# Another order table, and other durations in the planner, for a one-core transformer block

## The chip, the cores and the metric

The kernel runs on 1 core of one Trainium2 chip. A time is the device time of one execution in microseconds (us). An execution's time is a little longer than its span, which goes from the first to the last instruction of the trace. Five engines work side by side and meet at semaphores: TensorE (PE; its weight loads are shown apart as PEld), VectorE (DVE), ScalarE (ACT), GpSimd (POOL) and SyncE (SP), which here only issues transfers; its queue is shown as SPq.

## The reference

All is float32; x has 8 sequences of 512 tokens and 128 features. Cut to what matters:

```python
# attention: 16 heads of 64, 8 groups of keys and values, causal, all 512 tokens
q, k, v = x @ W_Q, x @ W_K, x @ W_V
probs = softmax(where(causal, q @ k.T / 8, -1e6))
x = layernorm(x + (probs @ v) @ W_out + b_out)
y = x
for l in range(2):                       # local layers
    h = shift_token(y)                   # half of the features come from the token before
    q, k, v = split(h @ wqkv[l], 3)      # 8 heads of 64
    q, k = rotary_xpos(l2norm(q) * qs[l], l2norm(k) * ks[l])
    # windows of 64 tokens, each sees itself and the window before, causal and at most 64 back
    y = y + local_softmax_attention(8 * q, k, v) @ wo[l]
    h = layernorm(shift_token(y)) * lg[l] + lb[l]
    a, g = split(h @ w1[l] + b1[l], 2)   # 341 each
    y = y + (a * gelu(g)) @ w2[l] + b2[l]
out = layernorm(x + y)
```

## The kernel before

**Steps.** The kernel first writes its work down as 5889 steps and emits nothing. A step is a call of `op(engine, us, fn, r=, w=, lat=, hold=, mode=)`: the engine, a listed duration, a function that emits some instructions, the buffers that it reads and writes, for a transfer the time until it has landed (`lat`), and for TensorE a tiling of the array (`mode`: WHOLE, ROWS, COLS or QUADS). `Plan.op` derives from the buffers which steps need which. There are 1264 steps on TensorE, 1744 on VectorE, 1384 on ScalarE, 993 on GpSimd and 504 on SyncE.

**The order.** `ORDER` is a table with the 5889 numbers of the steps, every one once. `Plan.run` walks it and calls each step's function; the tile framework's own scheduling is off (`manual_schedule`). So each engine gets its instructions in the order in which the table has its steps, and each engine works strictly in that order, SyncE's queue of transfers too. What an instruction has to wait for follows from the data and buffers, not from the table.

**Buffers.** `Plan.run` also keeps a small model of time. It uses the listed durations, `HOP` (a time per engine between a producer's end and the start of its reader), `TAIL` and `SWITCH`. This model does one thing in the emitted program: where a step needs a new buffer (one of 8 PSUM banks, or one of a few slots of a class such as `two`, `four`, `p3T`, `dram`), it takes the one that the model says is free first. Nothing is delayed or timed by it when the program runs.

**The stages of one sequence (a "batch", b = 0 to 7).** Attention: `heads` projects keys, queries and values (L828, L834, L843) for a pair of groups. `results` goes over the queries in three groups of 128-token tiles, (3), (2) and (0, 1): scores (L883, ROWS), mask and row minimum on VectorE (L895), exponentials with their sum on ScalarE (L907), reciprocal on VectorE (L915), normalization on GpSimd (L922). The weights must then be transposed. For tile pair (0, 1), and for all tiles of batch 0, TensorE does it (L935) and ScalarE or VectorE copies it back (L942). For tiles 3 and 2 of batches 1 to 7 VectorE transposes blocks of 32 x 32 (L957), a transfer stores them in DRAM (`leave`, L800) and four transfers read them back with the blocks in their new places (`come`, L804). Then come the values (L976, COLS), the output projection (L995) and a norm (`norm_rows`: transposition L754, statistics on VectorE L762 to L765, power on GpSimd L768, scaling on VectorE L775; `features` transposes back, L786).

Two local layers follow (`layer`): values (L1033), queries and keys (L1056), squares (L1063), norms, rotary (L1102, L1109, L1116, L1122 on VectorE and GpSimd), a transposition as above (L1156, L800, L804; in the last batch on TensorE, L1136), scores (L1183 and L1198, QUADS), softmax (L1219, L1224, L1230, L1232), transposition of the weights on TensorE (L1239, copied by L1242), outputs (L1251, COLS), projection (L1264), a norm, the feed-forward part (gate L1288, GELU L1295, other half L1303 with L1306, second matrix L1313 with L1319). At the end x is added (L1328), normed and stored (L1331).

The table interleaves the batches: the next batches' attention stands between the local layers of the batches before, and at the end of the table only batch 7 is left.

Of the kernel before, what the change touches and what calls it, by code (L numbers as in the profile page):

```python
# [16 lines left out]
PE, DVE, ACT, POOL, SP = range(5)  # L17
# [23 lines left out]
class Plan:  # L41
# [4 lines left out]
    HOP = (0.055, 0.034, 0.034, 0.085, 0.05)  # L46
# [91 lines left out]
    0, 66, 67, 258, 68, 76, 1, 82, 2, 12, 69, 7, 78, 77, 11, 13, 6, 9, 8, 10, 63, 80, 79, 83, 174,  # L138
    175, 187, 200, 194, 259, 808, 81, 215, 188, 16, 176, 177, 201, 195, 228, 241, 189, 207, 208, 32,
    28, 181, 190, 170, 235, 202, 216, 182, 56, 222, 203, 229, 223, 224, 191, 166, 178, 204, 49, 236,  # L140
    19, 183, 209, 184, 179, 210, 74, 171, 237, 180, 14, 196, 242, 230, 168, 72, 185, 225, 211, 3,
    226, 248, 238, 167, 197, 231, 73, 70, 192, 217, 218, 198, 169, 75, 27, 193, 199, 232, 186, 212,
    243, 233, 249, 2262, 219, 71, 220, 205, 206, 221, 172, 234, 173, 213, 244, 239, 250, 245, 240,
    251, 252, 53, 246, 18, 247, 138, 139, 227, 145, 40, 253, 22, 140, 125, 141, 142, 126, 46, 214,
    151, 158, 254, 127, 128, 143, 809, 132, 146, 159, 147, 152, 153, 129, 43, 110, 4, 144, 50, 97,
    160, 161, 148, 84, 154, 64, 111, 262, 104, 133, 134, 21, 155, 130, 135, 255, 47, 98, 85, 149,
    51, 810, 99, 86, 91, 92, 100, 162, 136, 263, 163, 156, 41, 87, 131, 137, 105, 117, 150, 106,
    260, 118, 157, 101, 93, 813, 119, 88, 112, 102, 89, 90, 103, 94, 164, 107, 113, 814, 95, 120,
    121, 122, 114, 115, 116, 108, 292, 165, 96, 52, 299, 109, 266, 293, 300, 267, 301, 294, 268,
    279, 286, 302, 295, 296, 123, 287, 280, 273, 303, 124, 320, 288, 289, 333, 307, 281, 23, 274,  # L150
    304, 269, 20, 270, 282, 327, 25, 297, 334, 335, 321, 322, 290, 291, 314, 275, 323, 283, 5, 276,
    315, 328, 44, 336, 340, 324, 256, 341, 325, 308, 329, 330, 316, 317, 284, 277, 309, 326, 271,
    310, 337, 342, 343, 278, 298, 331, 338, 272, 318, 344, 311, 332, 261, 285, 2989, 257, 305, 319,
    312, 345, 17, 45, 313, 339, 415, 422, 65, 423, 389, 306, 390, 416, 424, 59, 346, 402, 348, 396,
    391, 392, 24, 374, 425, 409, 417, 397, 393, 410, 403, 398, 418, 361, 29, 811, 55, 15, 355, 404,
    347, 349, 399, 419, 57, 362, 411, 412, 356, 357, 358, 405, 394, 264, 350, 375, 406, 413, 351,
    368, 363, 265, 395, 369, 352, 420, 58, 426, 427, 407, 815, 400, 414, 376, 364, 365, 370, 381,
    421, 359, 408, 816, 353, 371, 372, 401, 377, 812, 382, 366, 367, 428, 383, 378, 384, 373, 354,
    379, 380, 385, 61, 360, 62, 839, 844, 840, 386, 387, 827, 832, 866, 429, 388, 841, 878, 845,
    846, 842, 847, 60, 828, 833, 883, 884, 867, 885, 879, 868, 54, 871, 430, 829, 48, 42, 843, 848,  # L160
    872, 830, 1535, 26, 831, 851, 431, 38, 873, 834, 432, 880, 881, 823, 835, 890, 849, 886, 858,
    859, 882, 433, 852, 853, 825, 434, 897, 860, 861, 1536, 874, 909, 824, 898, 1537, 869, 435, 862,
    436, 870, 821, 437, 438, 887, 836, 891, 899, 888, 900, 439, 819, 854, 447, 892, 837, 37, 850,
    838, 875, 445, 893, 826, 855, 894, 876, 901, 456, 455, 453, 820, 454, 457, 910, 485, 889, 863,
    448, 561, 487, 446, 486, 562, 36, 488, 449, 856, 857, 895, 817, 450, 493, 489, 877, 902, 496,
    822, 525, 913, 451, 533, 490, 495, 914, 452, 458, 818, 864, 494, 918, 527, 526, 896, 491, 915,
    865, 937, 916, 497, 459, 919, 925, 944, 460, 920, 903, 534, 945, 930, 926, 528, 529, 563, 921,
    927, 440, 946, 931, 938, 904, 939, 964, 952, 461, 492, 463, 917, 928, 922, 441, 932, 976, 965,
    969, 966, 929, 911, 933, 947, 970, 934, 957, 1540, 530, 531, 566, 958, 977, 912, 907, 498, 948,
    971, 978, 983, 564, 959, 923, 967, 940, 532, 953, 972, 954, 535, 536, 968, 979, 935, 481, 565,  # L170
    905, 949, 2263, 955, 960, 499, 956, 462, 924, 908, 936, 464, 980, 941, 984, 906, 973, 482, 572,
    974, 961, 537, 538, 1541, 471, 567, 568, 942, 981, 569, 521, 943, 985, 950, 982, 465, 2264, 575,
    472, 574, 573, 962, 1001, 986, 473, 474, 1006, 501, 466, 467, 1025, 539, 522, 468, 1013, 951,
    1007, 987, 444, 570, 442, 500, 975, 1032, 995, 443, 963, 988, 484, 1002, 475, 541, 1008, 476,
    1003, 469, 1018, 1019, 1014, 1004, 1015, 1016, 1009, 1005, 1552, 989, 1026, 1020, 503, 470, 996,
    1017, 502, 990, 477, 1021, 1033, 1010, 1052, 540, 1022, 1053, 1034, 543, 1064, 1071, 478, 576,
    1040, 1054, 1057, 1023, 1065, 1058, 504, 511, 1059, 1045, 1538, 542, 1055, 1066, 1041, 571, 577,
    479, 1072, 991, 1073, 1011, 1056, 1027, 1028, 505, 1029, 480, 1042, 1035, 1043, 1067, 1060,
    1046, 1047, 523, 1539, 1061, 578, 1036, 512, 1048, 1074, 993, 1037, 1553, 1030, 994, 544, 513,
    1024, 1044, 1049, 1031, 545, 1012, 524, 483, 506, 551, 1038, 1062, 992, 514, 546, 552, 1079,  # L180
    1080, 1081, 1084, 1103, 553, 1068, 1091, 1085, 580, 507, 1092, 1093, 1050, 1063, 1104, 1082,
    1051, 31, 547, 1086, 1087, 1105, 999, 579, 508, 1546, 35, 515, 1069, 1083, 1110, 1070, 1075,
    997, 582, 1076, 1096, 1106, 1097, 1077, 1000, 516, 509, 1098, 1094, 1095, 1088, 1039, 998, 1118,
    1078, 1142, 510, 1089, 1099, 1100, 1101, 1123, 1130, 1111, 1119, 517, 554, 1124, 1135, 1107,
    1108, 1547, 581, 1112, 1125, 1126, 1136, 1131, 1542, 1113, 1149, 1143, 1120, 1132, 1144, 1543,
    1090, 1724, 555, 1109, 1102, 1121, 1122, 1114, 1133, 1636, 1550, 1137, 30, 1115, 1145, 1134,
    1127, 556, 1128, 1146, 1147, 1138, 1139, 1725, 518, 1148, 1140, 1150, 583, 584, 1116, 1551,
    1554, 590, 1151, 591, 1578, 592, 1555, 1129, 548, 1117, 1566, 1637, 585, 593, 1579, 1152, 1556,
    1634, 1153, 1585, 1544, 1635, 1154, 594, 1141, 1155, 1567, 1568, 586, 1557, 1558, 1559, 1569,
    549, 1605, 1571, 1560, 1572, 1570, 1586, 595, 1561, 1562, 1593, 1563, 1545, 1587, 1573, 1574,  # L190
    1156, 1610, 1575, 1594, 1580, 1617, 550, 587, 1581, 1618, 1588, 1624, 1625, 1598, 1599, 1564,
    1157, 1626, 1576, 39, 1565, 1158, 1582, 1583, 1600, 1595, 1596, 1611, 1589, 1590, 1606, 588,
    1159, 1601, 1612, 519, 1160, 589, 1607, 557, 1584, 596, 1577, 558, 1161, 33, 1597, 1613, 1162,
    1591, 1163, 1691, 1619, 520, 1164, 1608, 1602, 1592, 1627, 1609, 1614, 1603, 1679, 1166, 1615,
    1696, 1165, 1692, 1703, 1680, 597, 1693, 1620, 559, 1174, 1697, 1694, 1684, 1685, 560, 1695,
    1698, 1172, 1173, 1704, 1181, 1621, 1681, 1699, 598, 1175, 1686, 599, 1700, 1604, 1710, 1622,
    1548, 601, 1628, 600, 1167, 602, 1682, 1687, 1182, 1705, 1683, 1616, 1623, 1629, 1183, 603,
    1208, 1180, 1214, 1711, 1688, 1689, 1176, 604, 1712, 605, 1168, 1630, 1549, 1212, 1209, 1184,
    1177, 1631, 1652, 1215, 1701, 1702, 1664, 1640, 1178, 1213, 1653, 1690, 1706, 1654, 606, 1657,
    1179, 1658, 1671, 1672, 1641, 1185, 607, 1659, 1660, 1655, 1642, 1645, 1656, 1632, 1713, 1248,  # L200
    1665, 609, 1210, 1646, 1252, 1186, 610, 1643, 1647, 1644, 1714, 1249, 1648, 1666, 1673, 1638,
    1633, 1216, 1217, 608, 1187, 1707, 1661, 1715, 1649, 1260, 1218, 1639, 1708, 1253, 1188, 1709,
    1223, 1674, 612, 1716, 1211, 1222, 611, 1221, 1220, 1662, 1219, 1261, 1650, 1728, 1740, 613,
    1733, 1752, 1667, 1734, 1224, 1254, 1717, 1745, 1729, 1746, 1741, 1189, 1668, 1753, 614, 1262,
    1669, 1675, 1747, 1759, 1255, 1263, 1730, 1760, 1722, 1735, 1225, 1226, 1670, 1256, 1264, 616,
    1190, 1191, 1736, 1742, 1743, 1744, 1192, 1676, 1663, 617, 1754, 1755, 1731, 1732, 1756, 1651,
    1228, 1198, 1193, 1748, 1677, 2265, 1678, 2266, 1779, 1169, 615, 1723, 1791, 1784, 1199, 1792,
# [293 lines left out]
def kernel(  # L501
# [21 lines left out]
    nc = tc.nc  # L523
# [875 lines left out]
```

## Time and profile before

| | us |
|---|---|
| median of 3 runs | 1192.32 (1189.94 to 1193.11) |
| the profiled execution | 1189.79 |
| its span | 1188.0 |
| TensorE busy in the span | 1154.2 (97%) |
| VectorE, ScalarE, GpSimd busy | 952.6 (80%), 959.6 (81%), 891.4 (75%) |

The granted TensorE clock is 0.997 of full speed over the span. The transfers move 173.23 MB, at a mean of 146 GB/s.

How to read it: a row of groups shows the line, the engine, the operation, what it writes and reads, how often, its busy time, the mean of one in ns, and the idle time of the engine just before it with what ended that. A row of waits ("engine line <- what it waited for") shows the total in us, how often, and the longest. [...]

### The profile page before, as it was taken

How to read it: one execution, taken by the hardware profiler on the slowest of the kernel's cores; microseconds unless marked ns; L12 is line 12 of the kernel's file. 1: busy time of each engine (PE TensorE's matmuls, PEld its weight loads, DVE VectorE, ACT ScalarE, POOL GpSimd, SP SyncE). 2: the span in 40 equal slices, each digit the busy share in tenths (PEclk: the TensorE clock that was granted, in tenths of full speed). 3: DMA queues.
4: the chain of work that ended last, by engine and by line, in shares of the span. 5: the costliest groups of instructions: out<-in, count | busy, mean ns of one | idle time of the engine just before them, and what ended most of it. 6: DMA issues, size and time to landing. Idle time of an engine off the chain costs nothing.

```text
span 1188.0 us, 32813 instructions
## 1 busy us (share of the span) xinstructions
PE 1154.2 (97%) x11024; PEld 769.2 (65%) x11024; DVE 952.6 (80%) x2988; ACT 959.6 (81%) x3049; POOL 891.4 (75%) x1391
## 2 busy tenths in 40 slices
PE   8999999999999999999999999999999999999986
PEld 5775667566676667666576656766666676666672
DVE  3669967989887989888887888887889888968645
ACT  6867888888888878886898777887788887888783
POOL 3557955789777868778797579786879789989782
PEclk9999999999999999999999999999999999999998
DMA  7004775556655446555556535565456455203100
GB/s 190 15 2 146 241 246 156 178 178 191 196 166 178 162 140 200 174 145 170 160 172 179 188 127 168 159 190 159 157 179 194 136 161 170 81 2 109 36 2 27
DMA packets 180387, 173.23 MB, mean 146 GB/s; under 512 B 25682, under 2 KB 150780, under 8 KB 180220
## 3 DMA queue, kind: packets, MB, share of 16 engines
q1 hardware_dynamic: 178876, 170.35, 46.0%
q8 instruction: 89, 1.46, 0.5%
q10 hardware_dynamic: 1344, 0.79, 0.2%
q14 instruction: 78, 0.64, 0.2%
HBM read 88.22 MB, written 82.84 MB: 144 GB/s over the span
## 4 chain that ended last, share of the span: by engine, by line
PE 75%; DVE 7%; ACT 6%; DMA 4%; POOL 3%; SPq 2%; issue 2%; POOLq 0%; DVEq 0%; ACTq 0%
PE bank L883 11%; PE bank L976 10%; PE bank L1056 6%; PE bank L1251 4%; PE bank L1198 4%; PE bank L995 4%; PE bank L935 4%; PE bank L1264 4%; PE bank L1033 4%; PE bank L1239 4%; PE bank L834 3%; PE bank L1313 3%; PE bank L1303 3%; PE bank L1288 3%; SPq L804 2%
## 5 line engine op out<-in xcount | busy, mean ns | idle before, releaser
L922 POOL TENSOR_SCALAR p<-p,small 128x384 f32<-128x384 f32 (+3 forms) x512 | 264.9, 531 | 123.4 <-DVE small L915 91.8
L1224 ACT ACTIVATE weights<-bank,small 128x128 f32<-128x128 f32 x512 | 181.6, 383 | 27.2 <-DVE small L1219 25.8
L907 ACT ACTIVATE p<-bank,small 128x384 f32<-128x384 f32 (+1 forms) x224 | 142.4, 643 | 29.8 <-DVE small L895 22.4
L1116 POOL TENSOR_TENSOR four<-four,four 128x1024 f32<-128x1024 f32 x64 | 151.4, 2367 | 12.8 <-DVE four L1109 5.4
L1232 POOL TENSOR_TENSOR weights<-weights,small 128x512 f32<-128x512 f32 x128 | 132.3, 1039 | 37.6 <-DVE small L1230 30.3
L883 PE MATMUL bank<-four,four 64*128 64x384 f32 (+3 forms) x1024 | 160.1, 446 | 0.2 <-ACT four L985 0.2
L895 DVE CUSTOM_DVE_ANT_0 bank<-bank,cmask 128x384 f32<-128x384 f32 (+1 forms) x224 | 136.6, 635 | 25.2 <-PE bank L883 24.9
L907 ACT ACTIVATE p<-p,small 128x128 f32<-128x128 f32 (+3 forms) x288 | 135.7, 480 | 15.1 <-DVE small L895 14.8
L1122 POOL TENSOR_TENSOR four<-four,small 128x512 f32<-128x512 f32 x128 | 131.4, 1048 | 2.8
L957 DVE STREAM_TRANSPOSE p<-p 128x768 f32<-128x768 f32 (+1 forms) x112 | 122.4, 1100 | 10.5 <-POOL p L922 10.3
L1056 PE MATMUL bank<-wqkv_sb,hT 128*128 128x512 f32 x256 | 128.3, 601 | 0.2 <-ACT four L1063 0.2
L895 DVE CUSTOM_DVE_ANT_0 p<-bank,cmask 128x256 f32<-128x256 f32 (+3 forms) x288 | 97.4, 380 | 25.2 <-PE bank L883 23.8
L883 PEld LDWEIGHTS bank<-four,four 64*128 64x128 f32 x1024 | 82.8, 186 | 50.9 <-issue 17.1
L1224 ACT ACTIVATION_READ_ACCUMULATOR weights<-bank,small 128x1 f32 x512 | 114.1, 223 | 0.0
L1219 DVE TENSOR_REDUCE small<-bank 128x4 f32<-128x512 f32 x128 | 84.8, 680 | 23.7 <-PE bank L1198 17.6
L1109 DVE TENSOR_TENSOR four<-bank,tb 128x256 f32<-128x256 f32 x256 | 94.6, 414 | 11.4 <-ACT four L1063 6.7
L1102 DVE TENSOR_TENSOR four<-bank,ta 128x512 f32<-128x512 f32 x128 | 85.8, 679 | 13.9 <-ACT four L1063 9.3
L1156 DVE STREAM_TRANSPOSE four<-four 128x512 f32<-128x512 f32 x112 | 92.6, 909 | 2.3 <-POOL four L1122 2.3
L1063 ACT ACTIVATE four<-bank 128x512 f32<-128x512 f32 x128 | 75.4, 610 | 20.2 <-DVE four L1102 7.5
L1242 ACT COPY weights<-bank 128x512 f32<-128x512 f32 x128 | 74.0, 598 | 16.6 <-PE bank L1239 13.6
L1042 POOL COPY two<-two 64x512 f32<-64x512 f32 x128 | 77.2, 606 | 8.9 <-ACT two L1036 2.5
L1066 DVE TENSOR_REDUCE small<-four 128x8 f32<-128x512 f32 x128 | 80.5, 672 | 3.0 <-ACT four L1063 3.0
(104 smaller groups left out, 2692.9 us busy)
## 6 DMA issues: line engine op xcount, KB each, us to landing
dram<-p SPq DMA_DIRECT2D x56, 512.0 KB, 3.4
p4T<-dram SPq DMA_DIRECT2D x224, 128.0 KB, 3.0
dram<-four SPq DMA_DIRECT2D x112, 256.0 KB, 2.8
dram<-p SPq DMA_DIRECT2D x56, 384.0 KB, 2.7
p3T<-dram SPq DMA_DIRECT2D x224, 96.0 KB, 2.8
eight<-dram SPq DMA_DIRECT2D x224, 64.0 KB, 2.2
two<-dram SPq DMA_DIRECT2D x224, 64.0 KB, 2.3
two<-in_L_attn_resid_dram SPq DMA_DIRECT2D x8, 256.0 KB, 3.5
```

Of the source, the lines that this page charges most:

```text
L883: nc.tensor.matmul(s[j].t[:, ds(o, nk)], qT.t[ts(j, E), r, ts(t, P)], kv.t[ts(j, E), 0, :nk], start=True, stop=True,)
L895: nc.vector.tensor_tensor_reduce(s.t[:, :nk] if far else p.t[:, j, ds(o, nk)], s.t[:, ds(o, nk)], cmask[:, S - nk : S], 1.0, 3.0e38, ALU.a ...
L907: nc.scalar.activation(v, negated(p, s, j, o, nk), AF.Exp, bias=st.t[:, 2 * j + i : 2 * j + i + 1], scale=-1.0, accum_out=st.t[:, 8 + 2 * ...
L922: nc.gpsimd.tensor_scalar(v, v, st.t[:, 16 + 2 * j + i : 17 + 2 * j + i], 1.0, ALU.mult, ALU.mult,)
L957: op(DVE, 0.06 + 0.0021 * used, lambda p=p, flat=flat: nc.vector.transpose(flat(p), flat(p)), r=[p], w=[p])
L976: nc.tensor.matmul(pz.t[ts(j, E), ts(t, P)], kv.t[:, 1, ds(kb * P + j * E, E)], turned[:, j, kb] if far else p.t[:, j, ds(POFF[t] - POFF[f ...
L1056: nc.tensor.matmul(pq.t, hT.t[:, ts(t, P)], w if quick else w.rearrange("d (h e b) -> d e h b", e=2, b=B), start=True, stop=True,)
L1109: nc.vector.tensor_tensor(u[:, a], v[:, 1 - a], tb[:, l, t, s, ts(1 - a, B)].unsqueeze(1).broadcast_to([P, H, B]), ALU.mult,)
L1116: op(POOL, 2.35, lambda sw=sw, qn=qn: nc.gpsimd.tensor_tensor(qn.t, qn.t, sw.t, ALU.add), r=[qn, sw], w=[qn])
L1122: nc.gpsimd.tensor_tensor(split(qn.t[:, ts(s, HE)]), split(qn.t[:, ts(s, HE)]), y.unsqueeze(1).unsqueeze(3).broadcast_to([P, 2, H, B]), AL ...
L1224: nc.scalar.activation(weights()[:, c], s.t[:, ts(c, P)], AF.Exp, bias=part(0)[:, c : c + 1], accum_out=part(8)[:, c : c + 1],)
L1232: op(POOL, 1.05, lambda weights=weights, part=part: nc.gpsimd.tensor_tensor(weights(), weights(), spread(part(16)), ALU.mult), r=[(p, j), ...
```

## The change

It replaces the table `ORDER` by another permutation of the same 5889 steps, and changes listed durations, landing times and `HOP` in the planner. No step, instruction shape, buffer class or dependency is changed. The first difference is at the fourth place of the table; 5757 of the 5889 steps stand at another place, the middle one by 14 places. Within TensorE's own order 159 of the 1263 neighbouring pairs are kept.

```diff
-    HOP = (0.055, 0.034, 0.034, 0.085, 0.05)
+    HOP = (0.155, 0.054, 0.054, 0.1, 0.07)
...
 ORDER = [
-    0, 66, 67, 258, 68, 76, 1, 82, 2, 12, 69, 7, 78, 77, 11, 13, 6, 9, 8, 10, 63, 80, 79, 83, 174,
...
+    0, 66, 67, 68, 69, 2, 1, 7, 6, 10, 13, 11, 8, 258, 82, 83, 76, 77, 808, 78, 79, 80, 65, 259, 81,
...
-                        op(DVE, sum(0.065 + 0.00105 * a[1] for a in at), least, r=[s[j]],
+                        op(DVE, sum(0.075 + 0.00106 * a[1] for a in at), least, r=[s[j]],
...
-                        op(POOL, sum(0.15 + 0.0011 * a[1] for a in at), normalize,
+                        op(POOL, sum(0.25 + 0.00081 * a[1] for a in at), normalize,
...
-                        op(DVE, 0.06 + 0.0021 * used, lambda p=p, flat=flat: nc.vector.transpose(flat(p), flat(p)),
+                        op(DVE, 0.088 + 0.0021 * used, lambda p=p, flat=flat: nc.vector.transpose(flat(p), flat(p)),
...
                         op(SP, 0.47, lambda d=d, p=p, flat=flat, used=used: leave(d.t[:, : 2 * used], flat(p)),
-                           r=[p], w=[d], lat=2.7)
-                        op(SP, 1.85, lambda d=d, pT=pT, flat=flat, used=used: come(flat(pT), d.t[:, : 2 * used], used // 2),
-                           r=[d], w=[pT], lat=2.5)
+                           r=[p], w=[d], lat=3.4)
+                        op(SP, 2.0, lambda d=d, pT=pT, flat=flat, used=used: come(flat(pT), d.t[:, : 2 * used], used // 2),
+                           r=[d], w=[pT], lat=3.2)
...
-                       r=[sw], w=[d[s]], lat=2.3)
+                       r=[sw], w=[d[s]], lat=3.4)
...
-                       r=[d[s]], w=[(dst, t if s else None)], lat=2.1, hold=[qT, kT])
+                       r=[d[s]], w=[(dst, t if s else None)], lat=2.6, hold=[qT, kT])
```

`HOP` stands in the order TensorE, VectorE, ScalarE, GpSimd, SyncE. Eight more listed durations change by 0.02 to 0.15 us in the same way (copies, norms and rotary on GpSimd, a reduction and a reciprocal on VectorE, the local layers' reading back). Both tables change the tiling of TensorE between neighbouring steps: 381 times in the old one, 412 times in the new one. On SyncE the number of places from a store to the reading back of the same data is, for the attention weights, 1 (directly behind it) in 13 of 112 cases in the old table and 2 of 112 in the new one, with middle values of 3 and 3.5; for the local layers' queries and keys 1 in 24 and 11 of 112, with middle values of 3 and 4.

## The prediction

> **What bounds the kernel now.** I read, in this order, the page's busy times, the busy time by stage, TensorE's timeline at one place, the waits of TensorE, of its weight loads and of the DMA queue, and the transfers' landing times. TensorE (PE) is the bound:
>
> ```profile
> span 1188.0 us, 32813 instructions
> PE 1154.2 (97%) x11024; PEld 769.2 (65%) x11024; DVE 952.6 (80%) x2988; ACT 959.6 (81%) x3049; POOL 891.4 (75%) x1391
> ...
> 0.00:30.00 30.00, 24.43 (x143) 15.86 (x145) 11.22 (x53) 18.38 (x50) 9.79 (x26) 1.00 0.78 191
> 30.00:1110.00 1080.00, 1068.13 (x10318) 713.52 (x10315) 897.90 (x2803) 891.98 (x2859) 835.55 (x1307) 1.00 0.49 154
> 1110.00:1188.00 78.00, 61.68 (x568) 39.85 (x567) 43.46 (x133) 49.23 (x141) 46.09 (x60) 0.96 0.04 11
> ```
>
> In the stage rows the columns after the length are PE, PEld, DVE, ACT and POOL busy. Of PE's 33.8 us of idle time 5.6 lie in the first 30 us, 11.9 in the 1080 us of the middle, and 16.3 at the end, where one batch is left and nothing fills its waits. The middle looks full, but it isn't quite:
>
> ```profile
> 204.67 0.49 PE L935 MATMUL bank<-ident,p 128*128 128x128 f32 x3
> 205.00 1.02 PE L834 MATMUL bank<-two,wq_sb 128*128 128x512 f32 x2
> 205.86 0.49 PE L935 MATMUL bank<-ident,p 128*128 128x128 f32 x3
> 206.19 1.02 PE L1033 MATMUL bank<-wqkv_sb,hT 128*128 128x512 f32 x2
> 207.19 0.63 PE L754 MATMUL bank<-ident,hT 128*128 128x128 f32 x4
> ...
> 208.51 1.03 PE L1056 MATMUL bank<-wqkv_sb,hT 128*128 128x512 f32 x2
> 209.48 0.88 PE L976 MATMUL bank<-p,four 128*64 128x128 f32 x12
> ```
>
> Two 128x512 passes last 1.02 us, but the next step starts 0.86 us after them (205.00 to 205.86): 0.16 us of the last pass runs beside what follows. At 206.19 the next step comes 1.00 us later: 0.14 us were lost, and no idle time is listed. At 208.51 it comes 0.97 us later, because L976 uses the array in another tiling. So I took all start-to-start times of TensorE's 1264 steps from the trace and subtracted what the same kind of step takes undisturbed (the fast fifth of its kind, by the tiling of what follows). Lost time: 3.7 us to 30 us, 45.9 us in the middle, 14.0 us after 1110 us. In the middle 259 losses of 0.03 to 0.15 us are 22.6 us of it, and 48 larger ones another 22.6. A change of tiling costs 0.093 us (a two-pass step before the same tiling 0.861 us in the middle of 332, before another tiling 0.954 us of 52).
>
> ```profile
> PE bank L976 <- DMA p3T<-dram: 1.8, 1, 1.8
> PE bank L976 <- DMA p4T<-dram: 0.6, 2, 0.4
> PE bank L1198 <- DMA eight<-dram: 0.3, 1, 0.3
> PEld bank L935 <- POOL p L922: 11.2, 30, 1.5
> PEld bank L1239 <- POOL weights L1232: 5.0, 9, 1.0
> POOL p L922 <- DVE small L915: 91.8, 59, 6.0
> SPq L804 <- DMA dram<-four: 68.8, 35, 4.0
> SPq L804 <- DMA dram<-p: 60.9, 39, 3.7
> dram<-p SPq DMA_DIRECT2D x56, 512.0 KB, 3.4
> p4T<-dram SPq DMA_DIRECT2D x224, 128.0 KB, 3.0
> ```
>
> TensorE waits little for transfers (2.7 us listed), and more for the softmax chains that end on POOL. SyncE's queue (SPq) stands 130 us on its own stores.
>
> **The change, part by part.** The sum is made against the profiled execution's 1189.8 us (span 1188.0 and 1.8 around it); the median of the runs shown, 1192.3, is 0.21% above that, and I carry that over.
>
> *The constants* (hops, durations, landings) emit nothing. In the kernel they only choose which free buffer a step gets. That can move a wait on a buffer; it is in the bounds below.
>
> *Work.* All 5889 steps stay, each once, so matmuls, activations and the 173 MB of transfers stay: 0 us.
>
> *Tilings.* Written out step by step for TensorE, the old table changes the tiling 381 times, the new one 412 times. 31 x 0.093 = +2.9 us, on the engine that sets the end, hidden by nothing. [...]
>
> *Tight trips.* This is what the margin bears on. For each TensorE step that needs an earlier TensorE step through other engines (scores, minimum, exponentials, normalization, transposition) I counted the TensorE work that each table puts between the two and subtracted the chain's own listed durations; these serve to sort, not to time. Trips with under 1.5 us left, batches 1 to 6: 54 in the old table, 37 in the new one (-31%); under 3 us: 124 and 118 (-5%). Softmax transposition to the values' step (L935, L942, L976), under 1 us: 9 and 2. So the new table does give TensorE's inputs more time, where it was scarce. I take 31% off the small losses, which are the ones that a few tenths cure: 22.6 x 0.31 = -7.0 us; and 13%, nearer the 5%, off the larger ones, which come from queues and long chains: -3.0 us. Together -10. Both ends from the trace itself: its 21 stretches of 50 us from 50 to 1100 us lose 0.9 to 4.9 us each. If the whole middle ran like the best five (1.08 each) it would lose 23.3, a gain of 22.6 us; like the worst five (3.3) 71.3, a loss of 25.4 us.
>
> *Transfers.* SyncE works in its table's order, and a reading back stands until its store has landed. Readings that follow their own store at once: 13 and 24 of 112 each in the old table, 2 and 11 in the new one; the middle distance grows from 3 and 3 to 3.5 and 4 places. SPq's 130 us on its stores should shrink. Behind such a wait stand the next store (whose DVE transposition holds its buffer) and the next reading, for which L976 and L1198 wait; but TensorE's listed share is 2.7 us, so the gain is at most that, and it is in the larger losses. Moving readings later by one place (four issues; 1.75 us at 481.78 us of the timeline) can cost up to 1.75 us where no lead is left: bound +2 x 1.75, from the two longest such waits. Taken: 0.
>
> *The end.* In the last batch's last norm (L754 to L786) the old table puts 3.43 us of TensorE work under the 3.6 us of statistics, power and scaling; the new one 1.72. The rest was moved ahead, where the end loses time too (1110 to 1165 us: about 8 of the 14 us). Trips that can't fit add up to 5.2 us short in the old table and 6.6 in the new one: +1.4 us. Bounds 0 (all moved work fills another gap) and +1.7 us (none does).
>
> *The start.* The same steps in nearly the same order until 30 us; the loss there, 3.7 us, is waiting for the first tokens and their copy: 0, at most 1 either way.
>
> Sum: 1189.8 + 2.9 + 1.4 - 10.0 = 1184.1 us, 0.48% less; on the median's footing 1192.3 x 0.9952 = 1186.6, said as 1187.
>
> **The rivals.**
>
> *Losses only move.* Each input that comes earlier takes DVE, ACT or POOL time from another one; in the middle DVE is 83% and ACT 83% busy (897.9 and 892.0 of 1080). For it: the list of trips under 3 us hardly shrank. Against it: 17% of free time on each engine, and 17 fewer tight trips. Middle still 45.9: 1189.8 + 4.3 = 1194.1, on the median's footing 1196.6, slower by 0.36%. The counted costs alone are past 0.3% (the bound of what a measurement here tells from no change, 3.6 us), so it decides wherever the middle gains under 0.7 us.
>
> *The reciprocal behind a long DVE step.* POOL's L922 already waits 91.8 us for a reciprocal of 0.15 us (L915), which stands in DVE's queue behind transpositions of 1.23 us (L957). If the new table has them so more often, L935 gets its weights late: now 30 waits, 11.2 us; twice as many would be +11.2 us: 1205.3, or 1208. Against it: the trips from scores to L935 have at their scarce end (the 5% point) 4.5 us left instead of 3.8.
>
> *The margin works fully.* Half of the small losses and a third of the larger ones go: -11.3 - 7.5 = -18.8: 1175.3, or 1178. For it: losses of 0.03 to 0.15 us are just those that 0.1 us more on each input (HOP of PE from 0.055 to 0.155) would take away. Against it: 37 tight trips remain.
>
> *No effect beyond noise.* The middle gains 0.7 to 7.9 us: 1188.7 to 1195.9.
>
> **How the numbers follow.** The forecast (middle gains 8 to 15 us; 1182 to 1188.7) 0.40; the margin works fully (under 1182) 0.10; no effect 0.17; losses only move (1195.9 to 1202) 0.18; the reciprocal or another queue falls behind (above 1202) 0.15. Faster 0.50, same 0.17, slower 0.33. The bounds of the middle alone give 1174 to 1222; about 0.05 lies below 1174 and 0.12 above 1204, so the range is 1174 to 1204; the likeliest case's own is 1182 to 1189.
>
> **What would show it.** Right: steps of TensorE that change the tiling 31 more times; small losses near 180 instead of 259; SPq waiting clearly less than 130 us for stores; the end 1 to 2 us longer. Wrong: the middle's lost time at 46 us or more, PEld's waits for POOL L922 above 11 us, or waits for p3T, p4T or eight above 5 us. The forecast fails if the losses that I put down to short trips come from DVE's and POOL's queues or from buffers, which counting trips doesn't see.

## The result, and the profile after

| | before | after |
|---|---|---|
| median of the runs beside each other, us | 1191.60 (4 runs, 1189.94 to 1193.11) | 1208.84 (4 runs, 1207.70 to 1210.99) |
| the profiled execution, us | 1189.79 | 1209.79 |
| mean granted TensorE clock | 0.997 | 0.991 |

The ratio is 1.0147 with a 95% interval of 1.0125 to 1.0169: 1.5% slower. The forecast was 0.48% faster, with a range up to 1204.

The busy times of the page after, PE first:

```profile
span 1207.7 us, 32796 instructions
PE 1160.5 (96%) x11024; PEld 769.3 (64%) x11024; DVE 956.0 (79%) x2988; ACT 960.8 (80%) x3049; POOL 891.2 (74%) x1391
```

The stages after, with the columns as before (length, then PE, PEld, DVE, ACT and POOL busy, clock, DMA share, GB/s):

```profile
0.00:30.00 30.00, 24.07 (x145) 16.10 (x147) 10.60 (x52) 17.94 (x49) 12.23 (x33) 1.00 0.76 185
30.00:1110.00 1080.00, 1058.78 (x10155) 704.69 (x10152) 895.67 (x2792) 881.47 (x2822) 823.53 (x1288) 1.00 0.50 153
1110.00:1207.70 97.70, 77.65 (x732) 48.52 (x730) 49.77 (x145) 61.36 (x181) 55.41 (x72) 0.93 0.08 23
```

The work is the same (11024 matmuls, 173.23 MB moved), and every engine's busy time is within 0.6% of before. In the 1080 us of the middle PE now has 21.2 us of idle time instead of 11.9, and 163 matmuls fewer run in it. The last stage's clock fell from 0.96 to 0.93. So most of the time came in as waits of PE, in the middle as well as at the end. Of the waits of PE after (a row is "engine line <- engine buffer line that released it", then us in total, times, longest) these are the longest after the first tokens', and the longest for a transposition by transfer:

```profile
PE bank L1239 <- DVE two L1270: 3.0, 1, 3.0
PE bank L786 <- DVE two L775: 2.9, 1, 2.9
PE bank L1313 <- DVE hid L1306: 2.2, 1, 2.2
PE bank L754 <- POOL two L1328: 2.2, 1, 2.2
PE bank L883 <- ACT p L942: 2.2, 1, 2.2
PE bank L1239 <- ACT weights L1242: 1.6, 1, 1.6
...
PE bank L976 <- DMA p4T<-dram: 0.7, 1, 0.7
```

These rows are of two kinds. L786 reads what L775 wrote, L1313 what L1306 wrote, L754 what L1328 wrote: waits for data, all three at the end. But L1239 transposes softmax weights and reads nothing from L1270, which adds a projection to the residual; and L883 (scores) reads nothing from L942 (a copy of transposed weights). There the step waits for a *bank*: its data are there, and the PSUM bank that the planner gave it still holds a result that L1270 or L942 has not read. So is the wait for L1242, which copies what an earlier L1239 left in the bank. In the rows of before the longest wait for such a foreign pair is 1.2 us.

**Where the 19.2 us came in.** For each start of a TensorE step I took from the trace when its inputs were there and when its bank was free (the end of the last reader of what the bank held before). The later of the two names the loss; where both had been ready for over 0.45 us, the loss is "neither". A loss is the distance from the start of the step before, less the middle value of the same kind of step where nothing was late. "End" begins at the 1168th of the 1264 steps, at 1084 us before and 1098 us after.

| us | before | after | difference |
|---|---|---|---|
| first PE start | 4.9 | 5.3 | +0.4 |
| undisturbed steps of TensorE | 1130.1 | 1133.6 | +3.5 |
| loss until 30 us | 3.0 | 3.8 | +0.8 |
| loss in the middle | 27.8 | 37.9 | +10.1 |
| of it: bank / data / neither | 12.8 / 2.0 / 12.9 | 22.8 / 3.3 / 11.9 | +10.0 / +1.3 / -1.0 |
| loss at the end | 14.2 | 18.7 | +4.5 |
| of it: bank / data / neither | 0.6 / 10.7 / 3.0 | 5.2 / 11.9 / 1.6 | +4.6 / +1.2 / -1.4 |
| start of the last TensorE step | 1180.0 | 1199.2 | +19.2 |

Waiting for banks doubled, from 13.4 to 28.0 us. Losses to a bank of over 1 us were 2 in the middle before (2.7 us) and 9 after (14.9 us). The table shows one execution of each kernel, the experiments below what follows on the medians.

**What the table leaves in.** Its kinds of step, like the prediction's, are not parted by the tiling of the step *before* them. That misses half the price of a change of tiling. From the timeline before:

```profile
199.45 1.68 PE L883 MATMUL bank<-four,four 64*128 64x512 f32 x12
201.06 1.16 PE L1264 MATMUL bank<-two,wo_sb 128*128 128x128 f32 x8
202.06 1.88 PE L1056 MATMUL bank<-wqkv_sb,hT 128*128 128x512 f32 x4
203.78 1.05 PE L1264 MATMUL bank<-two,wo_sb 128*128 128x128 f32 x8
204.67 0.49 PE L935 MATMUL bank<-ident,p 128*128 128x128 f32 x3
```

L1264 stands here twice, and both times the step after it has the same tiling. The first one follows scores (L883, another tiling), and the next step starts 1.00 us after it; behind the second one it is 0.89. So in this trace a change of tiling makes the step ahead of it 0.09 us longer, which is the prediction's price, and the step behind it about 0.10 us as well (middle values of 0.05 to 0.10, by the kind). With kinds parted by the tilings on both sides, the undisturbed steps take 1132.2 us before and 1137.5 after (+5.3), and the middle loses 25.8 and 34.0 us (+8.2), 13.6 and 23.4 of it to banks. The losses to banks hardly depend on the baseline. Losses below go by the table's kinds where nothing else is said.

**One such wait.** From the timeline after (start, duration, engine and line; in brackets the idle time before it and its releaser):

```profile
340.81 1.50 PE L1264 MATMUL bank<-two,wo_sb 128*128 128x128 f32 x12
...
347.60 0.60 PE L1239 MATMUL bank<-ident,weights 128*128 128x128 f32 x4
...
348.28 0.60 ACT L1063 ACTIVATE four<-bank 128x512 f32<-128x512 f32 x1
...
348.92 0.69 DVE L1102 TENSOR_TENSOR four<-bank,ta 128x512 f32<-128x512 f32 x1 [3.47 <-ACT four L1063]
349.52 0.88 DVE L762 BATCH_NORM_STATS2 small<-bank 128x6 f32<-128x128 f32 x4
...
350.79 0.28 DVE L1270 TENSOR_TENSOR two<-bank,two 128x128 f32<-128x128 f32 x1
...
351.22 1.09 PE L1239 MATMUL bank<-ident,weights 128*128 128x128 f32 x4 [3.03 <-DVE two L1270]
```

The projection L1264 had written its bank by 342.3 us. Its reader L1270 needs 0.28 us, but the table puts it on VectorE behind L1102, which stood 3.47 us for ScalarE's L1063, and behind a norm's statistics. So the bank came free 8.8 us after it was written, and L1239, which had been given just this one, stood 3.03 us. In that time other banks were free: of all bank waits, 19.9 of 29.2 us after (9.5 of 14.6 before; positive losses only) had another bank whose last reader had ended earlier. The planner takes the first bank in its list that its *model* calls free (`free = max(s[1], now)`), and the model did not have this delay.

**The clock.** The same L1239 took 1.09 us instead of the 0.60 us at 347.60. The stretches around it after (length, PE, PEld, DVE, ACT, POOL busy, clock, DMA share, GB/s):

```profile
347.00:348.00 1.00, 1.00 (x11) 0.96 (x10) 0.00 (x0) 0.20 (x1) 0.58 (x2) 1.00 1.04 379
348.00:351.00 3.00, 0.20 (x2) 0.00 (x0) 2.05 (x12) 1.36 (x3) 0.03 (x1) 0.96 0.05 17
351.00:352.00 1.00, 0.78 (x4) 0.71 (x4) 1.00 (x2) 0.00 (x0) 1.00 (x2) 0.50 0.00 0
352.00:353.00 1.00, 1.00 (x10) 0.76 (x10) 1.00 (x4) 0.00 (x0) 1.00 (x2) 0.50 0.00 0
353.00:354.00 1.00, 1.00 (x12) 1.00 (x10) 1.00 (x5) 0.96 (x6) 1.00 (x1) 0.50 0.97 385
354.00:355.00 1.00, 1.00 (x21) 1.00 (x20) 1.00 (x3) 0.54 (x4) 1.00 (x3) 0.92 0.99 258
```

The granted clock fell to 0.50 and stayed there from 350.8 to 354.2 us, 3.4 us. It did so again at 927.6, behind the 2.2 us wait of L883, and from 1193.8 to the end. Before, it fell only at 1181.5, behind the last matmuls. So more was lost there than the length of the waits: in the middle the steps in the two phases, 3.4 us each, took 1.4 and 1.3 us longer than undisturbed ones.

### The profile page after: what moved, and what is told of

It reads as the page before. It is cut to its first block, busy times and chain, and to the rows that moved or that the text cites. A ratio compares the mean times of both kernels' runs of the same rounds, so it can differ in the third digit from the quotient of the medians.

```text
span 1207.7 us, 32796 instructions
## 1 busy us (share of the span) xinstructions
PE 1160.5 (96%) x11024; PEld 769.3 (64%) x11024; DVE 956.0 (79%) x2988; ACT 960.8 (80%) x3049; POOL 891.2 (74%) x1391
## 2 busy tenths in 40 slices
DMA packets 180387, 173.23 MB, mean 143 GB/s; under 512 B 25682, under 2 KB 150780, under 8 KB 180220
## 3 DMA queue, kind: packets, MB, share of 16 engines
q1 hardware_dynamic: 178876, 170.35, 45.9%
## 4 chain that ended last, share of the span: by engine, by line
PE 79%; DVE 8%; ACT 6%; issue 2%; DMA 2%; POOL 1%; SPq 1%; POOLq 0%; DVEq 0%; ACTq 0%
PE bank L883 12%; PE bank L976 11%; PE bank L1056 6%; PE bank L1251 5%; PE bank L995 4%; PE bank L1198 4%; PE bank L935 4%; PE bank L1264 4%; PE bank L834 4%; PE bank L1239 4%; PE bank L1033 4%; PE bank L1303 3%; PE bank L1313 3%; PE bank L1288 3%; PE bank L828 2%; ACT weights L1224 2%
## 5 line engine op out<-in xcount | busy, mean ns | idle before, releaser
L922 POOL TENSOR_SCALAR p<-p,small 128x256 f32<-128x256 f32 (+3 forms) x512 | 265.1, 531 | 144.7 <-DVE small L915 111.0
L1224 ACT ACTIVATE weights<-bank,small 128x128 f32<-128x128 f32 x512 | 181.6, 382 | 34.8 <-DVE small L1219 33.7
L907 ACT ACTIVATE p<-bank,small 128x512 f32<-128x512 f32 (+1 forms) x224 | 141.7, 637 | 41.2 <-DVE small L895 30.4
L883 PE MATMUL bank<-four,four 64*128 64x128 f32 (+3 forms) x1024 | 163.9, 450 | 3.0 <-ACT p L942 2.2
L895 DVE CUSTOM_DVE_ANT_0 bank<-bank,cmask 128x512 f32<-128x512 f32 (+1 forms) x224 | 136.8, 632 | 28.8 <-PE bank L883 27.9
L1232 POOL TENSOR_TENSOR weights<-weights,small 128x512 f32<-128x512 f32 x128 | 132.4, 1039 | 20.4 <-DVE small L1230 14.4
L907 ACT ACTIVATE p<-p,small 128x256 f32<-128x256 f32 (+3 forms) x288 | 135.4, 478 | 11.4 <-DVE small L895 11.2
L957 DVE STREAM_TRANSPOSE p<-p 128x768 f32<-128x768 f32 (+1 forms) x112 | 122.7, 1100 | 10.6 <-POOL p L922 10.1
L895 DVE CUSTOM_DVE_ANT_0 p<-bank,cmask 128x128 f32<-128x128 f32 (+3 forms) x288 | 97.1, 379 | 30.3 <-PE bank L883 24.7
L883 PEld LDWEIGHTS bank<-four,four 64*128 64x128 f32 x1024 | 82.6, 187 | 54.9 <-issue 15.2
L1224 ACT ACTIVATION_READ_ACCUMULATOR weights<-bank,small 128x1 f32 x512 | 113.1, 221 | 0.0
L1102 DVE TENSOR_TENSOR four<-bank,ta 128x512 f32<-128x512 f32 x128 | 85.4, 676 | 17.5 <-ACT four L1063 16.3
L1063 ACT ACTIVATE four<-bank 128x512 f32<-128x512 f32 x128 | 75.5, 611 | 28.8 <-DVE four L1102 13.3
L1242 ACT COPY weights<-bank 128x512 f32<-128x512 f32 x128 | 75.0, 597 | 15.8 <-PE bank L1239 13.9
L1239 PEld LDWEIGHTS bank<-ident,weights 128*128 128x128 f32 x512 | 59.5, 141 | 42.8 <-issue 25.5
```

Of the source, the lines that this page charges most:

```text
L883: nc.tensor.matmul(s[j].t[:, ds(o, nk)], qT.t[ts(j, E), r, ts(t, P)], kv.t[ts(j, E), 0, :nk], start=True, stop=True,)
L895: nc.vector.tensor_tensor_reduce(s.t[:, :nk] if far else p.t[:, j, ds(o, nk)], s.t[:, ds(o, nk)], cmask[:, S - nk : S], 1.0, 3.0e38, ALU.a ...
L907: nc.scalar.activation(v, negated(p, s, j, o, nk), AF.Exp, bias=st.t[:, 2 * j + i : 2 * j + i + 1], scale=-1.0, accum_out=st.t[:, 8 + 2 * ...
L922: nc.gpsimd.tensor_scalar(v, v, st.t[:, 16 + 2 * j + i : 17 + 2 * j + i], 1.0, ALU.mult, ALU.mult,)
L957: op(DVE, 0.088 + 0.0021 * used, lambda p=p, flat=flat: nc.vector.transpose(flat(p), flat(p)), r=[p], w=[p])
L1224: nc.scalar.activation(weights()[:, c], s.t[:, ts(c, P)], AF.Exp, bias=part(0)[:, c : c + 1], accum_out=part(8)[:, c : c + 1],)
```

## The experiments

Two theories: (1) the choice of banks makes the kernel slower, since planner and chip disagree on when a bank is free; (2) the new order itself does, wherever the banks are. Every ratio is against the kernel before in runs on the same chip.

**1. The banks by the trace, table after.** Each of the 1520 uses of a bank gets the free bank whose last reader ended first in the trace after. No step changes its place.

```diff
+        picks = iter(BANKS)
...
-                for s in self.slots[b.cls]:
+                if b.cls == BANK:
+                    s = self.slots[BANK][int(next(picks))]
+                    best = s[1], s
+                    assert s[2]
+                for s in self.slots[b.cls] if b.cls != BANK else ():
```

> The new table, but each of the 1520 uses of a PSUM bank gets, of the banks free at that place of the table, the one whose last reader ended first in the trace of the changed kernel. Theory 1 (the loss is TensorE waiting for a bank that the planner chose badly, while another was free): by the ends of the readers in that trace, waits for banks fall from 27.7 us to 9.4 us, so 1188 to 1194 us, and PE waits on L1270, L1242 and L1093 over 1 us vanish. Theory 2 (the new table has DVE's, ACT's and POOL's steps in a worse order; the bank is only where it shows): the late steps stay late and something else waits for them, 1203 to 1210 us.

1201.73 against 1189.19 us: 1.0107 (1.0092 to 1.0123), so 0.40% better than after. In its trace the waits for banks fall from 28.0 to 14.0 us, what they were before; waits for data grow by about 4 us. Waits of PE in this kernel (its lines are 24 higher: L1263 is L1239, L1256 is L1232, L810 is L786):

```profile
PE bank L1263 <- POOL weights L1256: 4.0, 4, 2.5
PE bank L1337 <- DVE hid L1330: 2.2, 1, 2.2
PE bank L810 <- DVE two L799: 1.9, 1, 1.9
```

The 3.0 us for L1270 are gone, and the largest rows are of data now. Both theories hold a part: banks alone don't explain the loss.

**2. The bank that is free longest, by the model.** The simple repair: the planner takes the bank that its own model freed first.

```diff
-                    free = max(s[1], now) if b.cls == BANK else s[1]
+                    free = s[1]
```

> The new table; the planner takes the bank that by its own model has been free longest, instead of the first one that it holds free by now. Theory 1: by the trace of the changed kernel, waits for banks fall from 27.7 to 19.8 us, so about 1201 us (1196 to 1205). Theory 2: 1205 to 1211 us.

1206.40: 1.0141 (1.0124 to 1.0157), no more than 0.06% from after. Waits for banks in the middle fall to 16.0 us, but losses with neither late rise to 16.1 and those for data to 4.5. Theory 1 missed here.

**3 and 4. Half of the change.** First the old table with the new constants, then the new table with the old constants. The constants emit nothing; they only feed the model that picks the buffers.

```diff
-    HOP = (0.055, 0.034, 0.034, 0.085, 0.05)
+    HOP = (0.155, 0.054, 0.054, 0.1, 0.07)
...
 ORDER = [
     0, 66, 67, 258, 68, 76, 1, 82, 2, 12, 69, 7, 78, 77, 11, 13, 6, 9, 8, 10, 63, 80, 79, 83, 174,
...
```

> The old table with the new constants, which emit nothing but choose buffers: 702 of 1520 bank uses get another bank. Theory 1: by the trace of before, waits for banks rise from 13.5 to 52.7 us if none overlap; 1205 to 1231 us. Theory 2 (the table's order is what costs): 1189 to 1195 us. The prediction's step that the constants cost nothing says the same, 1189 to 1195.

> The new table with the old constants; 498 of 1520 bank uses get another bank. Theory 1: by the trace of the changed kernel, waits for banks rise from 27.7 to 37.8 us, 1211 to 1222 us: a table goes only with the choice of banks that it was searched with. Theory 2: 1205 to 1211 us. A third one, that the new constants alone make the loss: 1189 to 1197 us.

Old table, new constants: 1214.91, 1.0217 (1.0200 to 1.0234). 702 of 1520 bank uses differ from before, each engine has its steps in the same order, and the kernel is 2.2% slower. The constants also move 265 of the 1618 uses of other buffers, but by the trace the engines wait little for those: 3.6 us in all, mostly in SyncE's queue, against 2.7 before. In the trace the middle's loss is 49.2 us instead of 27.8, and 33.8 instead of 12.8 of it are waits for banks; for about nine tenths of that time another bank had come free earlier. Waits of PE there:

```profile
PE bank L976 <- ACT weights L1242: 3.1, 3, 1.7
PE bank L976 <- ACT p L907: 1.5, 2, 1.1
PE bank L883 <- ACT weights L1224: 1.5, 3, 0.7
```

L976 (values) reads nothing from L1242 (a copy of local weights): foreign pairs again, and before the same three pairs are listed with 0.3 us or less, or not at all. No wait here is long and the clock stays at 0.998: many short waits make the sum. New table, old constants: 1216.33, 1.0231 (1.0216 to 1.0247); 498 uses differ from after, and the banks cost 26.2 us in the middle. So "constants emit nothing" does not mean that they cost nothing: with the other table's constants each of the two tables is slower, the old one by 2.17% and the new one by 0.84%.

**5 and 6. The end alone.** The old table to its 5545th place with the last 344 steps in the new order (old constants), and the reverse (new constants).

```diff
-    ... 5016, 5045, 5017, 5683, 5684, 5010, 5011, 4425, 5686, 4428, 4431, 4433, ...
+    ... 5045, 5119, 5683, 5684, 5685, 5010, 5016, 4425, 5017, 5046, 4988, 5065, ...
```

> The old table and constants up to the last layer of the last two batches (the first 5545 places, 1167 of TensorE's 1264 steps); what is left follows in the new table's order. By the two traces the new end is 4.5 to 5 us longer. If the end's order is at fault (the prediction's step: less work under the last norm, +1.4, at most +1.7), 1190.5 to 1191.5 us; if the trace's difference is the end's own, 1193.5 to 1195 us; if the end is long only because what comes before it is late, 1188 to 1190 us.

> The new table and constants with the old order for the same end. The changed kernel is at 1206.7 us on this footing (1.0147 x 1189.2): if the end is its own matter, 1201.5 to 1202.5 us; if not, 1206 to 1208.

The new end in the old table: 1196.31 against 1189.34, 1.0059 (1.0043 to 1.0075), or 7.0 us, more than any of the three outcomes had. Its loss at the end is 20.3 us instead of 14.2. The old end in the new table: 1205.20, 1.0132 (1.0117 to 1.0147), only 1.8 us better than after by the ratios, and the intervals overlap. What the end costs seems to depend on the banks that it gets: in this trace the old end waits 3.5 us for banks, in the kernel before 0.6. Experiment 10 returns to it. The end after, PE's timeline:

```profile
1176.18 0.63 PE L754 MATMUL bank<-ident,hT 128*128 128x128 f32 x4 [0.33 <-POOL hT L792]
1176.64 1.88 PE L1303 MATMUL bank<-two,w_sb 128*128 128x512 f32 x4
1181.37 0.66 PE L786 MATMUL bank<-ident,two 128*128 128x128 f32 x4 [2.85 <-DVE two L775]
1181.87 2.74 PE L1313 MATMUL bank<-hid,w_sb 128*128 128x512 f32 x6
...
1192.68 4.38 PE L1313 MATMUL bank<-hid,w_sb 128*128 128x512 f32 x6 [2.23 <-DVE hid L1306]
1199.24 1.12 PE L754 MATMUL bank<-ident,two 128*128 128x128 f32 x4 [2.18 <-POOL two L1328]
```

Between the norm's transposition L754 and L786 stand the four matmuls of L1303 (1.88 us), and PE then waits 2.85 us; before it had eight (1.02 and 2.74 us) there, and waited 0.53. In front of the last L1313 before stood two matmuls of L1313 itself, and PE waited 0.32 us there:

```profile
1164.41 0.66 PE L786 MATMUL bank<-ident,two 128*128 128x128 f32 x4 [0.53 <-DVE two L775]
...
1174.42 1.13 PE L1313 MATMUL bank<-hid,w_sb 128*128 128x512 f32 x2
1175.87 1.99 PE L1313 MATMUL bank<-hid,w_sb 128*128 128x512 f32 x4 [0.32 <-DVE hid L1306]
```

After, all six come together behind a wait of 2.23 us, and the last of them run at half clock (0.50 from 1193.8 us): 4.38 us instead of 2.74.

**7 and 8. The same repairs on the old table.** The bank list by the trace before, and the bank that is free longest.

```diff
+BANKS = (
+    "01234567023541673254031674320576157435160732156047132643501263470152743520173451027531473024530"
...
```

> The old table with each bank chosen by the ends of the readers in the trace of before. Theory 1 (a bank chosen better is time won): waits for banks 13.5 to 5.4 us by that trace; half of such a fall came through with the new table (14 us less waiting for banks, 9.1 us less span), so 1183 to 1186 us. Theory 2 (other waits take their place): 1187.5 to 1190 us.

> The old table; the planner takes the bank that its model has had free longest. By the trace of before, waits for banks 13.5 to 7.0 us: 1184 to 1187 us by theory 1, 1187.5 to 1192 us by theory 2.

1187.69 (0.9984, 0.9974 to 0.9993) and 1188.14 (0.9987, 0.9976 to 0.9998). In the first, waits for banks in all halve from 13.4 to 6.5 us, but those for data in the middle grow from 2.0 to 5.4: of 6.9 us, 1.7 reach the end. A PE that doesn't wait here comes sooner to the next step, whose input is not there yet.

**9. Eight late readers moved.** If single readers like L1270 above are the cause, then moving them ahead should cure it. Eight steps that read a bank late are moved forward in the table after; every use keeps its bank.

```diff
-    ..., 736, 1949, 2410, 2440, 1330, 662, 1331, ...
+    ..., 2427, 2428, 662, 1950, 2414, ...
```

> The new table and its own banks; only eight steps stand earlier in the table, the late readers of the banks that TensorE waits for longest in the middle (L1270 at 351 us, L942 at 927, L1242 at 747, L1093 at 610, L1306 at 1006, L849 and L942 at 107 and 110, L838 at 521 us): each goes ahead of the steps that it stood behind on DVE or ACT though its own data had been there for up to 8.5 us. These waits are 13.8 us, and two phases of 3.4 us at half the clock follow on the longest ones. If a late reader in an engine's queue is the cause, 1206.7 - 8 to - 15: 1192 to 1199 us, and no half clock in the middle; the one L1306 can't move far. If the waits only go elsewhere, 1203 to 1208 us.

1205.56 against 1190.57: 1.0121 (1.0103 to 1.0138), 0.26% (3.1 us) better than after by the ratios, with overlapping intervals. The 3.0 us wait is gone, and others stand at or near its place. PE's timeline in this kernel (L929 is L883, L1270 is L1224):

```profile
350.92 1.12 PE L929 MATMUL bank<-four,four 64*128 64x512 f32 x2 [0.25 <-DVE two L1316]
353.05 1.65 PE L929 MATMUL bank<-four,four 64*128 64x384 f32 x4 [1.01 <-ACT weights L1270]
```

At 352.7 us the clock fell to 0.50 again. The middle's loss goes from 37.9 to 35.6 us only. So the late reader was how that wait came about, not a cause that can be taken out by itself. It looks as if VectorE's and ScalarE's queues are late as a whole there; that is read from these two waits, not tested.

**10. Banks by the trace and the old end, in the new table.** Experiments 1 and 6 together.

> The new table with the banks of the first experiment and the old order of the end. If choice of banks and end add up: 1201.7 - 5 (trace: 18.8 against 13.8 us lost in the end with measured banks) = 1195.5 to 1198 us; what then remains over the old table with measured banks (1187.7) is the tilings (3.4) and 4 to 5 us of the middle. If the end is worth only what the old end gave on the new table before, 1199 to 1201 us.

1196.54: 1.0053 (1.0032 to 1.0074). So with these banks the new end's order costs 0.54%, about what experiment 5 found. The old table with banks chosen in the same way (experiment 7) is at 0.9984. The 0.69% between them, 8.2 us, are the part of the new order that is neither the end nor the choice of banks. In the traces it is 3.1 us more of undisturbed steps (1133.2 against 1130.1) and 5.5 us of loss in the middle (31.0 against 25.5). With kinds parted by the tilings on both sides it is 5.0 us of tilings and 3.5 us of loss. Waits for banks in the middle are 12.7 us here and 6.8 in experiment 7, so they are more than the whole of these 3.5 us. In both kernels at most 0.2 us of them had another bank that had come free earlier: in the new order TensorE more often comes to a step when none of the banks left to it is ready.

**11 and 12. A better one.** The old table with banks by experiment 7's trace, and the end in another order: the last feed-forward part of batch 7 sends its gate and other half (L1288, L1303) ahead of the last L1313 of batch 6, and its GELU result goes to a buffer of class `eight`. The twelfth kernel also moves four readers and three of SyncE's transfers.

```diff
-        hh = Buf("hid")
+        hh = Buf("eight", lambda t: t[:, : NCH * S].rearrange("p (c s) -> p c s", c=NCH)) if quick and l == L - 1 else Buf("hid")
```

> The old table with measured banks; in the last layer of the last batch the chain no longer waits behind batch 6's second matrix (L1313, 2.6 us): gate and other half of batch 7 come first, and that layer's GELU buffer lies in a free slot of another class. In the trace TensorE's gate steps start 2.9 us after their input (1163.3 to 1167.0 us with L1278 done at 1164.1). If that order is what bounds the end, 1.4 to 2.5 us off 1187.7: 1185 to 1186.5 us. If the last batch's GpSimd and DVE steps bound it anyway, 1187 to 1188.5.

> The same with four late readers (L1109 at 551 us, L1036 at 481, L1259 at 1147, L1242 at 1062) and three stores (before the 2.4 us loss at 801 us) at other places of their queues. Their losses are 6.3 us; if a third to a half comes through, 1182 to 1184.5 us; if not, as the run before, 1185 to 1187.

1186.99 (0.9970, 0.9957 to 0.9982) and 1186.52 (0.9963, 0.9950 to 0.9976). Both are faster than both kernels, by 0.3 to 0.4% against before. Against experiment 7 the eleventh is 0.14% faster, within the intervals, and what the twelfth adds can't be told from nothing. The end of the eleventh, PE's timeline (L1335, L1350 and L1360 are L1288, L1303 and L1313; L833 is L786):

```profile
1162.89 1.08 PE L833 MATMUL bank<-ident,two 128*128 128x128 f32 x4
1164.84 2.84 PE L1335 MATMUL bank<-two,w_sb 128*128 128x512 f32 x6 [0.87 <-ACT two L1325]
1167.52 2.74 PE L1350 MATMUL bank<-two,w_sb 128*128 128x512 f32 x6
1170.10 2.74 PE L1360 MATMUL bank<-hid,w_sb 128*128 128x512 f32 x6
1172.67 2.74 PE L1360 MATMUL bank<-eight,w_sb 128*128 128x512 f32 x6
```

From 1164.84 to 1175 the four steps stand without a gap, and the end's loss is 12.3 us instead of 13.8 in experiment 7.

## Why the prediction was wrong

**Tilings, +2.9 us: the sign right, the size wrong.** The price of 0.093 us is what the step ahead of a change loses. The step behind it loses 0.05 to 0.10 us more, and with both the undisturbed steps took 5.3 us more.

**The constants, nothing: wrong.** They were put into the bounds as what "can move a wait on a buffer", and the sum had 0. Experiment 3 shows that on the old table they alone cost 2.2%, by its trace nearly all through the choice of banks. That is over four times the gain that I had for the whole, in a term set to nothing. It can't be added to the cost of the new table: that one is slower still with the old constants (experiment 4).

**Tight trips, -10 us: the step that failed.** It took 7.0 us off the small losses and 3.0 off the larger ones; instead the middle lost 8 to 10 us more. By its own measure the small losses of the middle went from 22.4 to 21.5 us (255 to 251 of them), and the larger ones from 22.2 to 33.0 (46 both times). Two things were wrong in it.

First, the small losses were not what I took them for. My baseline, the fast fifth of a kind, put steps behind a change of tiling together with steps behind none: scores (L883) of 384 columns take 0.645 us in one piece between scores, and 0.749 us behind another tiling. A recount, with kinds a little wider, finds 237 of 280 small losses before (20.7 of 24.2 us) and 233 of 264 after at steps behind a change. Most small losses were thus the other half of the price of the tilings, which no earlier input takes away. With the table's baseline, the middle value of undisturbed steps, the middle before loses 27.8 us, not 45.9. Of these only 2.0 us are waits for inputs, which is all that a margin on inputs can win; 12.8 us are for banks and 12.9 have neither late. The trips did get longer, as counted, and PE's weight loads for L935 wait 5.4 us for L922 instead of 11.2. There was almost nothing to gain by it.

Second, counting trips sees data only. What grew was waiting for banks, from 12.8 to 22.8 us in the middle. The prediction named this as its way to fail ("from DVE's and POOL's queues or from buffers"), but gave it no price, though the rows of before let one sort the waits by whether the releaser is an input.

**The end, +1.4 us (0 to 1.7): the sign right, the size wrong.** It measured +4.5 us in the trace after and 7.0 us by itself (experiment 5). I counted the work under one norm; the wait in front of the last L1313, the banks (0.6 to 5.2 us) and the half clock behind such waits were not counted.

**The start, 0, at most 1: right.** The loss until 30 us grew by 0.8 us, and the first step came 0.4 us later.

**Transfers, 0: right.** SyncE's queue stood less on its own stores, as forecast; its waits after, and the landing times on the page after:

```profile
SPq L804 <- DMA dram<-four: 35.9, 26, 2.9
SPq L804 <- DMA dram<-p: 23.5, 21, 3.4
```

```profile
dram<-p SPq DMA_DIRECT2D x56, 512.0 KB, 2.8
p4T<-dram SPq DMA_DIRECT2D x224, 128.0 KB, 3.3
```

That is 59 us instead of 130, and it moved nothing: of PE's waits only 0.9 us are listed for such transfers, against 2.7.

**The rivals.** "Losses only move" had the right direction but no size for banks (1196.6). "The reciprocal behind a long DVE step" came to the right time (1208) by the wrong way. POOL's wait for it did grow, as the first of these rows after shows:

```profile
POOL p L922 <- DVE small L915: 111.0, 67, 14.2
PEld bank L935 <- POOL p L922: 5.4, 17, 0.8
```

But what was to follow, L935 waiting longer for L922, halved (second row; 11.2 us before). The range failed because its upper end came from the mechanisms that I had, and the bounds from the trace (up to 1222) were cut to 1204.

**The sum of the 1.47% (17.5 us)**, by the ratios above, each good to 0.2 or 0.3%: the choice of banks 0.40% (experiment 1), the end's order 0.54% (10 against 1), the rest of the order 0.53%. That rest is 0.69% against the old table with equally chosen banks; by the traces it is 5.0 us of tilings, and waits for banks where no other one had come free earlier.

**What stays open.** Why banks come free later for TensorE in the new order, even with the measured choice. The planner's new constants raise the margin for what TensorE reads (`HOP`, 0.055 to 0.155) and leave that for the release of a bank at 0.05 (`b.free = max(b.free, end + 0.05)`): an order searched with them can lean on a bank that comes free just in time. That is argued from the code; the search was not run anew with a margin on banks.

## What to carry to other kernels

Before a better order is given a price, sort the bound engine's lost time into waits for data, waits for a buffer and neither, with a baseline that keeps unlike steps apart, by the tilings on both sides of them too: only the first can shrink when inputs come earlier. Where a planner's model picks the buffers, its constants are part of the schedule, and a change of durations alone can cost more (2.2% here) than a new order may win. When a wait is taken away, look for what is late behind it: of 14.0 us of bank waits removed about 5 us reached the end in one kernel, and of 6.9 us 1.7 in the other.

## What was not expected of the hardware

In these traces a change of tiling cost TensorE 0.15 to 0.2 us, 0.09 of it in the step ahead and the rest in the step behind: in the middle, before and after, two-pass steps between steps of the same tiling take 0.86 us, ahead of a change 0.95, behind one 0.96, and between two changes 1.06 (middle values).

The granted clock was halved behind some of TensorE's waits, for 3.4 us at a time or longer. After: 3.0 us of standing, and 0.50 from 350.8 to 354.2; 2.2 us, and 0.50 from 927.6 to 931.0. In experiments 2, 4 and 6 (mean clocks of 0.990, 0.989 and 0.993 in the profiled executions) a wait near the place of the first one was followed by 6.8 us at 0.50. Not each such wait was followed by it: at the end of after, 2.85 us of standing until 1181.4 left the clock at 1.00, and so did 2.2 us until 801.2 in experiment 7. And shorter ones were: in experiment 9 it fell at 352.7 behind waits of 0.25 and 1.01 us. When the clock fell, PE had stood for 2.6 us at the first place in after (since 348.2) and for 0.7 us in experiment 9 (since 352.0). Before, the middle had no wait over 2 us, and the clock stayed at 1.00 there. Among the six executions of experiment 5 the two with a mean clock of 0.996 took 1194.3 and 1194.8 us, the two with 0.994 1194.6 and 1197.8, the two with 0.991 1198.2 and 1198.6: the same kernel was granted more or less of its clock. What decides whether a wait is followed by half the clock is not shown by these runs.

The 1.00 of the first stage's row leaves something out: in before the record of the clock begins at 10.7 us; from 7.68 to 10.24 the passes of L828 start 0.85 us apart, and the one at 10.92 is followed after 0.43.
